# A vision tower with mixture of experts on one core: tokens' join and the first norm's copy on ScalarE, the expert choice ahead of the second differences, and another order in the last block

## The chip, the core and the metric

The kernel runs on one core of a Trainium2 chip. The core has five engines that run beside each other, each with its own queue of instructions: PE (TensorE, matrix products), DVE (VectorE), ACT (ScalarE), POOL (GpSimd) and SP (SyncE, which here only issues DMA transfers). An instruction waits on semaphores until what it reads is there and what it writes is free; everything behind it on the same engine then waits too. The metric is the device time of one execution in microseconds (us); lower is better. The time before is the median of three executions, 2139.51 us (2135.47 to 2140.91).

## The reference

The input is 4 images of 64 channels x 512 steps x 64 columns. A tokenizer makes 16384 tokens of 256 features; an attention-like block with a decaying sum over time and a small perceptron follows, then a layer of 8 experts of which each token takes two.

```python
def _L0_tok_ref(x, W):
    ...
    xf = jnp.fft.rfft(patches, axis=-2, norm='ortho')
    ...
    x_emb = jnp.concatenate([x_real, x_imag], axis=-1)
    x_emb = x_emb @ W.T

def _L0_attn_ref(x, ...):
    h = _layernorm(x, ln1_g, ln1_b)
    q = h @ Wq.T + bq
    k = h @ Wk.T + bk
    v = h @ Wv.T + bv
    def step(mem, inp):
        kv_t, q_t = inp
        mem = decay * mem + kv_t
        return (mem, q_t * mem)
    ...
    x = x + ret
    h2 = _layernorm(x, ln2_g, ln2_b)
    mlp = relu(h2 @ W1.T + b1) @ W2.T + b2
    return x + mlp

def _moe(tokens, router_w, w1, b1, w2, b2):
    probs = softmax(tokens @ router_w.T)
    rw, re = jax.lax.top_k(probs, TOP_K)          # two of eight
    rw = rw / jnp.maximum(rw.sum(-1, keepdims=True), 1e-12)
    out = tokens
    for e in range(E):
        h = gelu(tokens @ w1[e] + b1[e])
        out = out + combine[:, e:e + 1] * (h @ w2[e] + b2[e])

h = _L0_tok_ref(x, W)
h = h + _L0_attn_ref(_layernorm(h), ...)
h = h + _moe(_layernorm(h), ...)
```

## The kernel before

**Blocks.** The tokens are worked on in 32 blocks of 512 (`NB`, `BLK`; the last one's index is `NS` = 31). A block passes through three stages, and one turn of the main loop holds three blocks: `new` = block i, `mid` = block i − 1, `old` = block i − 2.

- `new`: `embed` makes 20 products of five difference planes `xv` with the folded tokenizer weights `wu` (L391) and combines them to `h` on DVE; it then makes two norms of `h` with the same statistics, `zz` (normalized twice, what the projections read) and `z` (normalized once, what the residual adds to), both on DVE by `Norm.apply` (L287, four instructions of 128x256 each). `zz` is turned to feature order `hT`, then `qkv` makes the projections with seven products each for q, k and v (a Strassen-Winograd scheme: `mix_tokens` on DVE makes sums of token halves, L488 to L491; the products are L504, L519 and L520). `scan` runs the decaying sum on DVE (L566, L567, L577), `residual` transposes it back on PE (L588) and adds `z` (L591).
- `mid`: `features2` joins its turned tokens on ACT, `mlp_in` (L334, ACT's relu L620) and `mlp_out` (L630) are the perceptron, and the last norm gives `tok`.
- `old`: `rows` writes the tokens and their numbers as rows (ACT, L678), `turn3` and `join3` turn them to `tokT`, `logits` (L703) scores the experts, `choose` (L727 to L746) picks two of them on DVE, `place` counts the places (PE, L773) and makes the shares (L751 to L754), and `scatter` sends each row to its two experts' regions of a buffer in HBM (POOL, L796). `store` writes the block to the output.

**Turning.** `Turn.split` makes two planes of 16-bit halves on ACT (L313), `start` issues a transposing DMA on SP (L321) into the tile `turned`, and `join` puts the halves together with four copies of 128x512 16-bit elements (L327). `turned` and `planes` have a single buffer: a transfer for the next turn waits until the join before it is done. The first `EARLY` = 6 blocks and the last one turn `zz` with PE's transposes (L300) instead.

**Differences.** The five planes `xv` of the block after `new` are made on DVE by the generator `differences` (L363, L366) in two parts: before its first `yield` four instructions, and then five more. In the loop both parts stand at m = 5 of the perceptron's eight steps, around `features1` and `mix_tokens`. The block after that is loaded into `xb`, a single buffer, by `load_x` on SP.

**Tiles.** A tile is 256 routed rows of one expert. In each turn a few tiles go through their expert between the steps of the blocks ("slots"): SP loads weights, turned rows and shares; ACT puts the rows together (`turn`, L972); PE multiplies twice (`enter`, L979, with gelu on ACT, L987, and `leave`, L996); DVE adds the bias and scales (`sums`, L1008 to L1015, into `y`, four buffers); POOL adds the result to the output with two indirect accumulating transfers a tile (L1025), each waiting for the last two before it to land. After the loop only tiles remain, and the last block's tokens go through all experts densely (L1058 to L1089).

**Order.** The engines PE, DVE, ACT and SP run their instructions in the order in which the program writes them; the order on POOL follows from dependencies. At the turn of the main loop (L1153 on) `join3` stands ahead of the eight steps `mlp_in`; at m = 1 `new.split1()` follows; after the eight steps `logits` and `choose` come, the steps of `qkv` with a tile between them, `place`, `scan`, `mlp_out(0)`, `residual` and `mlp_out(1)`. Blocks 29 to 31 end in a section of its own behind the loop, where `last` is block 31, with its tiles taken by `expert_step` and `expert_halves`.

Of the kernel before, what the change touches and what calls it, by code (L numbers as in the profile page):

```python
# [20 lines left out]
P = 128  # L21
# [15 lines left out]
def vit_tower_kernel(  # L37
# [203 lines left out]
    def mix_weights():  # L241
# [5 lines left out]
        nc.vector.tensor_tensor(t4, w[:, :, 1, 0], t2, ALU.subtract)  # L247
        nc.vector.tensor_tensor(w[:, :, 0, 1], w[:, :, 1, 1], w[:, :, 0, 1], ALU.subtract)

    class Norm:  # L250


# [92 lines left out]
    class Block:  # L345
# [34 lines left out]
        def embed(self):  # L380


            xv = self.xv.rearrange("p i (j w) n -> p i j (w n)", j=J)
            self.h = three.tile([P, TT, D], F32, name="h")
            h = [self.h[:, t, :] for t in range(TT)]

            def products(which):
                ps = p_tm.tile([P, 2, D], F32, name="tm")
                for n, i in enumerate(which):
                    for j in range(J):  # L390
                        nc.tensor.matmul(  # L391
                            ps[:, n, :], lhsT=xv[:, i, j, :], rhs=wu[:, i, j, :], start=j == 0, stop=j == J - 1
                        )
                return ps

            def scaled(to, a, by, b, op):
                nc.vector.scalar_tensor_tensor(to, a, by, b, ALU.mult, op)

            ab = emb.tile([P, 2, D], F32, name="ab")
            nc.scalar.copy(ab, products((1, 2)))  # L400
            a, b = ab[:, 0, :], ab[:, 1, :]
            p, q = h[0], h[3]
            scaled(p, b, 1.0 / 3, a, ALU.add)
            scaled(q, b, -1.0 / 3, a, ALU.add)
            yield
            ps = products((3, 0))
            c, m0 = ps[:, 0, :], ps[:, 1, :]
            norm = Norm()
            scaled(h[2], c, 2.0 / 3, p, ALU.subtract)
            scaled(h[1], c, 1.0 / 3, q, ALU.subtract)  # L410
            scaled(h[0], m0, 0.5, p, ALU.subtract)
            scaled(h[0], c, 1.0 / 6, h[0], ALU.add)
            scaled(h[3], c, 4.0 / 3, q, ALU.subtract)
            for t in range(TT - 1):
                norm.stats(self.h, t)
            yield
            nc.vector.tensor_tensor(h[3], products((4,))[:, 0, :], h[3], ALU.add)
            norm.stats(self.h, TT - 1)
            norm.factors(twice=True)
            yield  # L420
            self.z = one.tile([P, TT, D], F32, name="z")
            self.zz = one.tile([P, TT, D], F32, name="zz")
            norm.apply(self.zz, self.h, 1)
            norm.apply(self.z, self.h, 0)

        def split1(self):
            if self.i < EARLY:
# [259 lines left out]
            self.turn = Turn()  # L687
            self.turn.start([self.row.bitcast(U16)[:, t, : 2 * D] for t in range(TT)])

        def join3(self):  # L690
            self.tokT = one.tile([P, KD, BLK], F32, name="tokT")
            self.turn.join(self.tokT, nc.vector.tensor_copy)

        def features3(self):
            self.tokT = one.tile([P, KD, BLK], F32, name="tokT")
# [16 lines left out]
        def choose(self):  # L712

            ps = self.lg
            shape = [P, TT, E]

            def wide(a):
                return a.unsqueeze(2).to_broadcast(shape)

            lg = small.tile(shape, F32, name="lg")  # L720
            top = small.tile([P, TT], F32, name="top")
            if self.i == NS:
                first_key = small.tile([P, TT], F32, name="first_key")
            else:
                first_key = self.row.bitcast(F32)[:, :, FIRST]
            turned = small.tile([P, TT, G], F32, name="turned_lg")
            nc.vector.transpose(turned.rearrange("p t g -> p (t g)"), ps.rearrange("p t g -> p (t g)"))  # L727
            nc.vector.tensor_reduce(top, turned[:, :, :E], AX.X, ALU.max)
            nc.vector.tensor_tensor(lg, turned[:, :, :E], wide(top), ALU.subtract)
            key = small.tile(shape, F32, name="key")  # L730
            self.oh = oh = small.tile([P, 2, TT, E], F32, name="oh")
            nc.vector.scalar_tensor_tensor(key, lg, 0.0, key0, ALU.is_equal, ALU.mult)
            nc.vector.tensor_reduce(first_key, key, AX.X, ALU.max)
            nc.vector.tensor_tensor(oh[:, 0], key, wide(first_key), ALU.is_equal)
            nc.vector.scalar_tensor_tensor(lg, oh[:, 0], -3.0e38, lg, ALU.mult, ALU.add)
            second = small.tile([P, TT], F32, name="second")
            nc.vector.tensor_reduce(second, lg, AX.X, ALU.max)
            nc.vector.tensor_tensor(key, lg, wide(second), ALU.is_equal)
            nc.vector.tensor_tensor(key, key, key0, ALU.mult)
            nc.vector.tensor_reduce(top, key, AX.X, ALU.max)  # L740
            nc.vector.tensor_tensor(oh[:, 1], key, wide(top), ALU.is_equal)
            dtype = F32 if self.i == NS else BF16
            self.both = small.tile(shape, dtype, name=f"both_{dtype.name}")
            nc.vector.tensor_tensor(self.both, oh[:, 0], oh[:, 1], ALU.add)
            self.ex = small.tile([P, TT], F32, name="ex")
            nc.gpsimd.tensor_tensor(self.ex, euler, second, ALU.pow)  # L746

        def weights(self, diff, second):

# [374 lines left out]
    def run(steps):  # L1124
        for _ in steps:
            pass

    def expert_step(**how):
        run(expert_halves(**how))
# [19 lines left out]
    with tc.manual_schedule(engines=MANUAL):  # L1149
# [3 lines left out]
        for i in range(NS):  # L1153
# [22 lines left out]
            next(embed, None)  # L1176
            if at["enter"]:
                slot(known, load=False)
            if old:
                old.join3()  # L1180
            for m in range(KH):
                if mid:
                    mid.mlp_in(m)
                if m == 1:
                    new.split1()

                    if at["enter"]:
                        advance("load", at["enter"] + AHEAD - 1)
                    elif known > 1:
                        advance("turn", 2)  # L1190
                if m == TT - 1:
                    slot(known)
                if m == KH // 2 and old:
                    old.store()
                if m == KH - 3:
                    ahead = blocks[i + 1].differences(xs.pop(i + 1))
                    next(ahead)
                    new.features1()
                    if i:
                        new.mix_tokens()  # L1200
                    next(ahead)
            if i == NS - 1:
                slot(known)
            later = iter(())
            if i:
                qkv = new.qkv()
                if old:
                    old.logits()
                    old.choose()
                next(qkv)  # L1210
                next(qkv)
                tile_steps = slot_halves(known, sums=False)
# [3 lines left out]
                    writes = old.place(at_once=False)  # L1216
                    old.scatter(1)
                run(tile_steps)
                if i + 2 < NB:
                    xs[i + 2] = load_x(i + 2)  # L1220
                if old:
                    old.scatter(2, last_product[0])
                next(qkv)
# [1 line left out]
                later = slot_halves(known, load=False)  # L1225
                next(later, None)
                next(qkv)
                for m in range(KD):
                    new.scan(m)
                mid.mlp_out(0)  # L1230
                if old:
                    old.scatter(3, last_product[0])
            else:
                xs[i + 2] = load_x(i + 2)
                for m in range(KD):
                    new.retention(m)
            new.residual()
            run(later)
            if old:
                old.scatter(4, last_product[0])  # L1240
            if i == 0:
                mix_weights()
            else:
                new.split2()
            if at["enter"]:
                advance("load", at["enter"] + AHEAD - 1)
            if mid:
# [15 lines left out]
        next(embed, None)  # L1263
        expert_step()
        weights = load_bank()
        old.join3()
        for m in range(KH):
            mid.mlp_in(m)
            if m in (1, 3, 5, 7):
# [2 lines left out]
                expert_step()  # L1272
            if m == KH - 3:
                last.features1()
                last.mix_tokens()
        next(weights)
        old.logits()
        old.choose()
        expert_step()
        writes = old.place()  # L1280
        next(weights)
        qkv = last.qkv()
        next(qkv)
        next(qkv)
        out_steps = mid.mlp_out_steps(0)
        next(out_steps)
        next(qkv)
        run(out_steps)
        next(weights)
        take(NS - 1, old, writes)  # L1290
        next(qkv)
        next(weights)
        expert_step()
        next(qkv)
        for m in range(KD):
            last.scan(m)
        mid.mlp_out(1)
        expert_step(fetch=False, sums=False)
        joined = last.residual_steps()
        next(joined)  # L1300
        beside = expert_halves(fetch=False, sums=False)
        next(beside)
        mid.features3()
        mid.rows()
        run(beside)
        mid.logits()
        mid.choose()
        advance("sums", at["leave"] - 1)
        expert_step(fetch=False, sums=False)
        writes = mid.place()  # L1310
        run(joined)
        expert_step(fetch=False, sums=False)
        advance("sums", at["leave"] - 1)
        take(NS, mid, writes)

        last.features2()
# [118 lines left out]
```

## Time and profile before

| what | value |
|---|---|
| median of three executions | 2139.51 us |
| the profiled execution: its time, its span | 2141.64 us, 2139.9 us |
| mean granted clock of PE in it | 0.993 |
| one turn of the loop, from one issue of the row transposes to the next (1007.87 to 1070.27) | 62.4 us |
| DVE, L327 `tokT`: 120 copies | 44.1 us, 451 ns each |
| DVE, L287 `z` from `h`: 128 instructions | 44.0 us, 407 ns each |
| ACT, L327 `hT`: 100 copies | 66.2 us, 762 ns each |
| ACT, L663 (identity with scale and bias, 128x256): 124 | 64.0 us, 590 ns each |
| POOL, L1025: 226 accumulating transfers for routed tiles | 386.6 us, 1711 ns each |
| DVE small operation on 128x4, L272 | 0.16 us |
| ACT, loading a function table | 2 times, 1283 ns each |

The profiled execution lies 2.1 us above the median. Its span is what the profiler's records cover; 1.7 us lie around it. A row of the timeline gives the start, the duration from the first to the last instruction of a group, the engine, the line, the output and input, the shape, and in brackets how long the engine had been idle just before it and what released it. Idle time of an engine costs nothing unless the work that sets the end waits for it. The granted clock is 1.00 at full speed.

### The profile page before, as it was taken

Reading aid. Unit: us, or ns where it says so; the run is one execution under the profiler, and the core shown is the slowest. Engines: PE = TensorE matmul, PEld = TensorE weight load, DVE = VectorE, ACT = ScalarE, POOL = GpSimd, SP = SyncE. Lnnn points to the kernel's source line nnn. Section 1 sums busy time; section 2 is a strip of 40 time slices with the busy share of each in tenths; the row PEclk is TensorE's granted clock in tenths of the full one; section 3 lists DMA queues with packets and bytes.
Section 4 is the critical chain, followed back from the end, with each engine's and each line's share of the span. In section 5 each row is a group of like instructions: output and inputs, shape, how many; then the busy total and the mean of one; then the engine's idle time right before and its main releaser. Section 6 shows DMA issues by size and latency. Waiting matters only on the chain.

```text
span 2139.9 us, 30460 instructions
## 1 busy us (share of the span) xinstructions
PE 2080.6 (97%) x9060; PEld 1580.7 (74%) x9060; DVE 1759.5 (82%) x5397; ACT 978.0 (46%) x1732; POOL 893.3 (42%) x769
## 2 busy tenths in 40 slices
PE   8999999999999999999999999999999999999988
PEld 6777677777777777777777777777777777776866
DVE  7888888888888888888888888888888888868544
ACT  1333344554444455444445544444555434554533
POOL 1022334444444444444444444444444444434444
PEclk9999999999999999999999999999999999999999
DMA  4032246776567677666767665676775566785643
GB/s 140 21 107 77 80 117 138 160 156 123 119 154 155 141 161 148 122 133 153 158 137 161 153 117 133 153 156 139 164 150 118 135 150 147 151 219 136 102 60 50
DMA packets 424519, 283.21 MB, mean 132 GB/s; under 512 B 355104, under 2 KB 391072, under 8 KB 420256
## 3 DMA queue, kind: packets, MB, share of 16 engines
q1 hardware_dynamic: 373424, 208.35, 41.6%
q0 software_dynamic: 49632, 67.39, 17.7%
q10 hardware_dynamic: 1296, 5.52, 0.7%
q8 instruction: 71, 1.16, 0.2%
q14 instruction: 96, 0.79, 0.1%
HBM read 118.36 MB, written 86.52 MB: 96 GB/s over the span
## 4 chain that ended last, share of the span: by engine, by line
PE 72%; DVE 16%; DMA 8%; issue 2%; POOL 1%; ACT 0%; SPq 0%; POOLq 0%; DVEq 0%; ACTq 0%
PE tm L630 19%; PE tm L391 12%; PE sums L334 12%; PE tm L996 10%; PE mm L979 8%; DMA turned<-planes 7%; PE sums L504 6%; DVE xv L366 2%; DVE xv L363 2%; DVE hT L327 2%; PE tm L588 1%; DMA out<-y,known 1%; PE tm L1075 1%; PE mm L1058 1%; DMA xh<-xbuf 1%
## 5 line engine op out<-in xcount | busy, mean ns | idle before, releaser
L1025 POOL DMA_INDIRECT out<-y,xg x226 | 386.6, 1711 | 454.6 <-DVE y L1015 258.0
L630 PE MATMUL tm<-w_sb,aT 128*128 128x256 f32 x2048 | 454.7, 380 | 0.0
L334 PE MATMUL sums<-hT,w_sb 128*128 128x512 f32 x1024 | 450.2, 592 | 0.0
L630 PEld LDWEIGHTS tm<-w_sb,aT 128*128 128x128 f32 x2048 | 386.7, 190 | 56.4 <-DVE z L591 4.5
L334 PEld LDWEIGHTS sums<-hT,w_sb 128*128 128x128 f32 x1024 | 194.1, 190 | 216.4 <-issue 205.2
L796 POOL DMA_INDIRECT xbuf<-row,to x248 | 245.6, 990 | 230.1 <-DVE row L754 89.1
L313 ACT COPY planes<-zz 128x1024 uint16<-128x1024 uint16 x100 | 99.6, 1043 | 451.4 <-DVE zz L287 451.4
L391 PE MATMUL tm<-wu,xv 128*128 128x256 f32 x1280 | 282.5, 379 | 0.0
L391 PEld LDWEIGHTS tm<-wu,xv 128*128 128x128 f32 x1280 | 242.7, 190 | 32.7
L996 PE MATMUL tm<-w,ge 128*128 128x256 f32 x1048 | 254.4, 386 | 6.8 <-DVE y L1013 6.8
L979 PE MATMUL mm<-xT,w 128*128 128x256 f32 x1048 | 249.9, 382 | 0.0
L979 PEld LDWEIGHTS mm<-xT,w 128*128 128x128 f32 x1048 | 200.1, 191 | 40.8 <-issue 14.5
L620 ACT ACTIVATE aT<-sums,vec 128x512 f32<-128x512 f32 x256 | 171.9, 683 | 117.4 <-PE sums L334 115.7
L996 PEld LDWEIGHTS tm<-w,ge 128*128 128x128 f32 x1048 | 196.1, 191 | 39.0 <-issue 10.5
L972 ACT COPY xT<-xh 128x512 uint16<-128x512 uint16 x262 | 182.3, 768 | 31.1 <-DMA xh<-xbuf 29.9
L987 ACT ACTIVATE ge<-mm,w 128x256 f32<-128x256 f32 x262 | 109.7, 474 | 153.3 <-PE mm L979 117.1
L278 POOL TENSOR_SCALAR rstd<-mv 128x4 f32<-128x4 f32 x62 | 42.0, 677 | 318.9 <-DVE mv L259 292.2
L1013 DVE TENSOR_TENSOR y<-tm,w 128x512 f32<-128x512 f32 x131 | 90.6, 691 | 45.7 <-PE tm L996 41.3
L504 PE MATMUL sums<-hT,wqkv_sb 128*128 128x256 f32 x372 | 110.7, 379 | 0.0
L258 DVE BATCH_NORM_STATS2 st<-h 128x6 f32<-128x256 f32 x256 | 104.8, 409 | 3.3
L366 DVE TENSOR_TENSOR xv<-xb 128x512 f32<-128x512 f32 x160 | 104.1, 683 | 3.1 <-DMA xb<-in_x 3.1
L327 ACT COPY hT<-turned 128x512 uint16<-128x512 uint16 x100 | 66.2, 762 | 81.4 <-DMA turned<-planes 81.4
(218 smaller groups left out, 3029.6 us busy)
## 6 DMA issues: line engine op xcount, KB each, us to landing
w<-in_wex SPq DMA_DIRECT2D x113, 641.5 KB
xb<-in_x SPq DMA_DIRECT2D x32, 1040.0 KB
out<-h SPq DMA_DIRECT2D x31, 512.0 KB
bank<-in_wex ACTq DMA_DIRECT2D x8, 641.5 KB
xbuf<-row,to POOLq DMA_INDIRECT x248
out<-y,xg POOLq DMA_INDIRECT x226
xh<-xbuf SPq DMA_TRANSPOSE x131
xg<-xbuf SPq DMA_DIRECT2D x131, 4.0 KB
```

What stands on the lines that cost most here:

```text
L334: nc.tensor.matmul(ps, lhsT=w[:, k, ts(m, P)], rhs=rhs[:, k, :], start=k == 0, stop=k == KD - 1)
L366: nc.vector.tensor_tensor(to, a, b, ALU.subtract)
L391: nc.tensor.matmul(ps[:, n, :], lhsT=xv[:, i, j, :], rhs=wu[:, i, j, :], start=j == 0, stop=j == J - 1)
L504: nc.tensor.matmul(g[:, n, :], lhsT=lhsT, rhs=rhs, start=False, stop=True, skip_group_check=True)
L620: nc.scalar.activation(self.aT[:, m, :], ps, AF.Relu, bias=vec[:, MB1 + m : MB1 + m + 1])
L630: last_product[0] = nc.tensor.matmul(ps[:, i, :], lhsT=self.aT[:, k, ts(u * 2 + i, P)], rhs=w2_sb[:, k, :], start=k == 0, stop=k == KH - 1,)
L796: write = nc.gpsimd.indirect_dma_start(out=xbuf, out_offset=bass.IndirectOffsetOnAxis(ap=self.to[:, c, t : t + 1], axis=0), in_=self.row[: ...
L972: nc.scalar.copy(halves[:, :, :, 1 - i], self.xh[:, i * KD : (i + 1) * KD, :])
L979: nc.tensor.matmul(ps[:, m, :], lhsT=self.w[:, k * D + m * P : k * D + (m + 1) * P], rhs=self.xT[:, k, :], start=k == 0, stop=k == KD - 1,)
L987: nc.scalar.activation(self.ge[:, m, :], ps[:, m, :], AF.Gelu, bias=self.w[:, 5 * D + m : 5 * D + m + 1])
L996: last_product[0] = nc.tensor.matmul(ps[:, c, :], lhsT=self.ge[:, k, ts(c, P)], rhs=w[:, (2 + k) * D : (3 + k) * D], start=k == 0, stop=k ...
L1025: add = nc.gpsimd.indirect_dma_start(out=out, out_offset=bass.IndirectOffsetOnAxis(ap=number[:, c, :], axis=0), in_=y[:, c, :], in_offset= ...
```

## The change

The change has five parts.

1. `join3` takes the copy as an argument. In the loop it is ACT's; the call moves from ahead of the eight steps to m = 1, ahead of `split1` (for i from `EARLY` on), or to m = 4, ahead of `store` (before that). The section behind the loop keeps DVE's.
2. `embed` makes `zz` on DVE as before, and in place of `z` one small operation for −mean/deviation; the new `first_norm` makes `z` with four ACT instructions, after the steps of `qkv`.
3. `next(ahead)`, the second part of the differences, moves from m = 5 to behind `choose` (i from `EARLY` on) or behind `residual` (0 < i < `EARLY`); the loads of `xb` move along in the program.
4. `choose` of the last block takes the exponential with ACT's function instead of POOL's power.
5. The last block makes its projections with `retention`, which block 0 uses too: four products for each half of the features instead of the seven, on weights whose last mixing step `restore_weights` undoes. `mix_tokens` is left out there, and the tile steps, `mlp_out` and the residual of the ending stand in another order.

```diff
+    def restore_weights():
+        w = wqkv_sb.rearrange("p w k (m q) -> p w k m q", q=P)
+        nc.vector.tensor_tensor(w[:, :, 0, 1], w[:, :, 1, 1], w[:, :, 0, 1], ALU.subtract)
...
             norm.apply(self.zz, self.h, 1)
-            norm.apply(self.z, self.h, 0)
+            self.first = norm
+            self.shift = small.tile([P, TT], F32, name="shift")
+            nc.vector.scalar_tensor_tensor(
+                self.shift, norm.mv[:, :, 0], -1.0, norm.rstd[:, 0, :], ALU.mult, ALU.mult
+            )
+
+        def first_norm(self):
+            for t in range(TT):
+                nc.scalar.activation(
+                    self.z[:, t, :],
+                    self.h[:, t, :],
+                    AF.Identity,
+                    bias=self.shift[:, t : t + 1],
+                    scale=self.first.rstd[:, 0, t : t + 1],
+                )
...
-        def join3(self):
+        def join3(self, copy):
             self.tokT = one.tile([P, KD, BLK], F32, name="tokT")
-            self.turn.join(self.tokT, nc.vector.tensor_copy)
+            self.turn.join(self.tokT, copy)
...
-            nc.gpsimd.tensor_tensor(self.ex, euler, second, ALU.pow)
+            if self.i == NS:
+                nc.scalar.activation(self.ex, second, AF.Exp)
+            else:
+                nc.gpsimd.tensor_tensor(self.ex, euler, second, ALU.pow)
...
-            if old:
-                old.join3()
             for m in range(KH):
                 if mid:
                     mid.mlp_in(m)
                 if m == 1:
+                    if old and i >= EARLY:
+                        old.join3(nc.scalar.copy)
                     new.split1()
...
                 if m == KH // 2 and old:
+                    if i < EARLY:
+                        old.join3(nc.scalar.copy)
                     old.store()
                 if m == KH - 3:
                     ahead = blocks[i + 1].differences(xs.pop(i + 1))
...
                     if i:
                         new.mix_tokens()
-                    next(ahead)
+                    else:
+                        next(ahead)
...
                     old.choose()
+                if i >= EARLY:
+                    next(ahead)
                 next(qkv)
...
                 next(qkv)
+                new.first_norm()
                 for m in range(KD):
                     new.scan(m)
+                if EARLY <= i < NB - 2:
+                    xs[i + 2] = load_x(i + 2)
...
             new.residual()
+            if 0 < i < EARLY:
+                next(ahead)
...
                 last.features1()
-                last.mix_tokens()
...
         writes = old.place()
         next(weights)
-        qkv = last.qkv()
-        next(qkv)
-        next(qkv)
-        out_steps = mid.mlp_out_steps(0)
-        next(out_steps)
-        next(qkv)
-        run(out_steps)
+        restore_weights()
+        last.first_norm()
+        last.retention(0)
+        mid.mlp_out(0)
         next(weights)
         take(NS - 1, old, writes)
-        next(qkv)
         next(weights)
-        expert_step()
-        next(qkv)
-        for m in range(KD):
-            last.scan(m)
         mid.mlp_out(1)
-        expert_step(fetch=False, sums=False)
-        joined = last.residual_steps()
-        next(joined)
-        beside = expert_halves(fetch=False, sums=False)
+        last.retention(1)
+        beside = expert_halves(fetch=False)
         next(beside)
         mid.features3()
         mid.rows()
-        run(beside)
+        advance("leave", at["enter"] - 1)
         mid.logits()
         mid.choose()
-        advance("sums", at["leave"] - 1)
+        run(beside)
         expert_step(fetch=False, sums=False)
         writes = mid.place()
-        run(joined)
+        advance("sums", at["leave"])
         expert_step(fetch=False, sums=False)
-        advance("sums", at["leave"] - 1)
+        last.residual()
+        expert_step(fetch=False, sums=False)
+        advance("sums", at["leave"])
+        expert_step(fetch=False)
         take(NS, mid, writes)
```

More of the change, by code (lines that the diff above doesn't have):

```diff
@@ L1218, in vit_tower_kernel @@
                 run(tile_steps)
-                if i + 2 < NB:
-                    xs[i + 2] = load_x(i + 2)
                 if old:
@@ L1234, in vit_tower_kernel @@
                 xs[i + 2] = load_x(i + 2)
+                new.first_norm()
                 for m in range(KD):
@@ L1244, in vit_tower_kernel @@
                 new.split2()
+            if 0 < i < EARLY:
+                xs[i + 2] = load_x(i + 2)
             if at["enter"]:
@@ L1265, in vit_tower_kernel @@
         weights = load_bank()
-        old.join3()
+        old.join3(nc.vector.tensor_copy)
         for m in range(KH):
```

## The prediction

> **What bounds the kernel now.** I read the page's busy times first, then the list of waits over the whole span, then one block of the loop engine by engine, then the end on POOL.
>
> ```profile
> span 2139.9 us, 30460 instructions
> PE 2080.6 (97%) x9060; PEld 1580.7 (74%) x9060; DVE 1759.5 (82%) x5397; ACT 978.0 (46%) x1732; POOL 893.3 (42%) x769
> ```
>
> PE is busy for 97% of the span: a faster step elsewhere is worth only the time in which PE stands still for it. The waits (engine, line, releaser; total us, times, longest) price these:
>
> ```profile
> DVE hT L327 <- DMA turned<-planes: 41.4, 25, 3.2
> PE tm L773 <- DVE both_bfloat L744: 15.6, 26, 1.7
> DVE share L751 <- POOL ex L746: 9.5, 1, 9.5
> PE tm L996 <- DVE y L1013: 6.8, 1, 6.8
> PE mm L520 <- DVE planes L488: 5.9, 17, 0.5
> ```
>
> PE waits 15.6 us in 26 blocks for the expert choice (L744), and 5.9 us for token sums that follow the join of hT; with the window cut to 56 to 1850 us, L519 adds 4.1 us in 5 blocks for hT itself. The two waits of 9.5 and 6.8 are one event at 2046. The timelines of one block (start, duration, instruction, then the idle before it) show the order that makes the waits:
>
> ```profile
> 1017.87 1.46 DVE L327 COPY tokT<-turned 128x512 uint16<-128x512 uint16 x4
> ...
> 1024.92 1.47 DVE L327 COPY hT<-turned 128x512 uint16<-128x512 uint16 x4 [1.36 <-DMA turned<-planes]
> ...
> 1027.97 1.28 DVE L366 TENSOR_TENSOR xv<-xb 128x512 f32<-128x512 f32 x2
> ...
> 1034.03 0.19 DVE L744 TENSOR_TENSOR both_bfloat<-oh 128x32 bf16<-128x32 f32 x1
> ```
>
> ```profile
> 1034.27 0.20 PE L773 MATMUL tm<-both_bfloat,rc 128*128 128x32 bf16 x2 [0.56 <-DVE both_bfloat L744]
> ```
>
> DVE makes the second half of the differences (1027.97 to 1031.2) before the choice (1031.22 to 1034.2), and PE arrives 0.56 us too soon. SP and ACT in the same block:
>
> ```profile
> 1007.87 5.13 SPq L321 DMA_TRANSPOSE turned<-row  x4
> 1019.39 3.31 SPq L321 DMA_TRANSPOSE turned<-planes  x1
> ```
>
> ```profile
> 1003.35 2.65 ACT L327 COPY hT<-turned 128x512 uint16<-128x512 uint16 x4 [2.88 <-DMA turned<-planes]
> ...
> 1015.13 1.99 ACT L313 COPY planes<-zz 128x1024 uint16<-128x1024 uint16 x2 [2.49 <-DVE zz L287]
> ```
>
> The planes were ready at 1017.12, but their transpose went out at 1019.39, just after DVE's tokT join: both use the single buffer `turned`. The end is POOL's:
>
> ```profile
> 1965.33 1.60 POOL L1025 DMA_INDIRECT out<-y,xg  x1 [0.30 <-DVE from_row L874]
> ...
> 2132.44 1.58 POOL L1025 DMA_INDIRECT out<-y,known  x1 [2.72 <-DVE zz L1083]
> ```
>
> Between these two lie 24 intervals of accumulate pairs, (2132.44 − 1965.33)/24 = 6.96 us each; the span ends 5.9 us after the last one starts.
>
> **Choice ahead of the second differences.** Nothing is added. The choice is 2.95 us long and the differences 3.25 (1027.97 to 1031.22), so L744 comes 3.25 us sooner against a longest wait of 1.7: the wait goes whole in the blocks from EARLY on. Late next is the place chain, which stands behind the differences on DVE: L773's result has 2.4 us of small operations before L540 at 1037.27, where DVE waited 0.36 for PE, so it fits within some 0.3 us. Scatters follow `place` on POOL and the following load of xb stands on SP at 1039.35, after both halves are made in either order. Value −15.0 (bounds −15.6 and −9, the last if each of 25 blocks keeps a quarter of a microsecond).
>
> **Early blocks.** In blocks 1 to 5 the second half moves behind the residual, where 3.25 us of DVE work delay the norm zz, and with it PE's transposes L300. Before, such transposes lost 4.0 us once up to 400 us. PE has other products queued ahead, and I take 0.3 a block, +1.5; bounds 0 and 5 x 3.25 = 16.3.
>
> **tokT join on ACT.** DVE loses four copies of 1.47 us in all. ACT gains four like the join of hT that it does already, 2.65 us. They stand after aT(1) (ends 1012.65) and ahead of the planes' copies. When are the rows there? DVE's join did not wait at 1017.87, which bounds the landing from above; the last issue ends at 1013.0. The windows of one microsecond (PE, PEld, DVE, ACT, POOL busy, clock, then DMA share and GB/s) say more:
>
> ```profile
> 1013.00:1014.00 1.00, 1.00 (x4) 0.48 (x3) 0.34 (x2) 0.00 (x0) 0.63 (x1) 1.00 0.64 130
> 1014.00:1015.00 1.00, 1.00 (x4) 0.47 (x3) 1.00 (x5) 0.00 (x0) 0.00 (x0) 1.00 0.00 0
> ```
>
> Packets stop at 1014, so with a little for the notice the copies run from 1014.3 to 1016.95. Planes follow to 1018.95, and SP issues at about 1019.0, 0.4 before the 1019.39 of today. Bounds: rows already there at 1012.65 leave the planes waiting for zz (1015.04), and SP issues at 1017.35, 2.0 sooner; rows there only at 1017.87 give 1020.5, 1022.5 and SP 3.2 later. I take the value by the DMA row, the nearest. In hT that is 0.3 to 0.4 us in each of the 17 blocks where L520 waited 0.35 on average; against it stand blocks where zz comes sooner than the rows and the issue slips. Value −3 of 10.0 us; bounds −10 and 25 x 3.2 = +80, the last a rival. aT(2) is next behind the planes on ACT: it would end at 18.95 + 0.69, 1019.65; the three sums buffers make m = 5 wait for it, and those products begin at 1018.64 + 1.72 = 1020.36. The cover is 0.7 us.
>
> **First norm on ACT.** DVE loses four of 0.41 (1.37 together) and gains one small operation of about 0.16 like L272. ACT gains four like L663, 2.07 us, from 1042.6 where it is idle until 1058; their reader L591 comes after the scans. Value 0; without that cover 2.07 x 31 = 64 us. Both moves free DVE of 31 x (1.37 + 1.47 − 0.16) = 83 us, worth nothing by themselves, and bring ACT from 978 to 978 + 31 x (2.65 + 2.07) = 1124, 53%.
>
> By the rows, moving this work costs 31 x (1.18 + 0.70) = 58 us of engine time and none of PE's. A rule speaks against it: the Trainium skill, "ScalarE: Activation LUTs", section "Rules for kernel authors", gives plain adds and products to VectorE. Its reason, that VectorE is faster for each element, is true of the rows: 1.47 against 2.65 us, 1.37 against 2.07. Taken as time on the path it would turn the sum below to plus 40; with ACT at 46% and DVE at 82% ahead of PE's waits, I go by the waits.
>
> **Ending.** Exp on ACT instead of POOL's pow takes away the 6.8 us at 2046 and the half clock around it (a mean of 0.51 from 2043 to 2050), but in that stretch POOL's accumulates, not PE, set the end: 0, or −10 if they did not. It brings two table loads; the trace's row for one is 1.28 us, 2.6 together, under the same cover. By the same page ("What ACT_TABLE_LOAD costs") a switch is 2.66 with its drain, and two would be 5.3; no run here shows a switch in mid kernel. In the last block twelve products of 128x512 at 0.86 (10.3) replace 21 of 128x256 at 0.43 (9.1). Two tile steps of 3.45 and some transposes leave the stretch from the first `place` to the second, 42.5 us today (1908.27 to 1950.77). In the new order I count 10.3 + 13.8 (64 rows of L630) + 1.7 + 1.6 + 1.7 + 0.6 + 1.7 + 1.7 = 33.1 us. So the second scatter comes about 9 us sooner, but one more pair of 6.96 stands behind it: −2. If it instead waits 3.5 us for zz or xT before `place` (such waits of 2.5 and 1.3 stand at 1957 and 1960 now), +1.5; a scatter not earlier at all, +7; a pair that finds its slot free, −7.
>
> **Sum.** −15.0 + 1.5 − 3.0 + 0 − 2.0 = −18.5 on the profiled execution (2139.9 and 1.7 around the span, 2141.6): 2123.1. It stood 2.1 above the median 2139.51, so the forecast is 2121.
>
> **Rivals.** *Eaten*: hT slips by 0.56 a block, as if the copies began 1 us later (rows noticed at 1015.3), 25 x 0.56 = 14: −15 + 14 + 1.5 − 2 = −1.5, 2138. For it: blocks with rows late against zz exist, and earlier accumulates on POOL may meet the transposes' packets. Against: packets end at 1014. *Slower*: the ACT join waits for the rows until past 1016, and planes, SP issue and hT all slip by 1.2 us or more: 25 x 1.2 = 30 (the 0.9 by which aT(2) then outruns its cover is part of it, since PE stands still once for both); −15 + 30 + 1.5 − 2 = +14.5, 2154. It decides from 0.8 us of slip on (−15.5 + 25 x 0.8 = +4.5); the spread of landings decides, and there is one buffer. It can grow by the clock: where the wait reached 1.4 us, the granted clock from 525 to 530 and 1714 to 1719 averaged 0.75 and 0.66; a like stretch in each of 25 blocks, 3.4 us at half speed, would add 25 x 1.7 = 42. *More*: every L519/L520 wait goes too (10.0), the ending keeps 7, early blocks cost nothing: −15.6 − 10 − 7 = −33, 2107. *The choice is not ahead in fact*: the order on DVE is written by hand, so the new program has it; no chance apart.
>
> **How the numbers follow.** Forecast 0.61 (its own range 2112 to 2133), more 0.12, eaten 0.11, slower 0.16. A measurement here tells 0.3%, 6.4 us, from no change. Faster is forecast and more, 0.73; same 0.11; slower 0.16. Range 2108 to 2143: it leaves out the slower case and the lowest few of "more".
>
> **What would show it.** L773's wait under 1 us in all; DVE L327 left with hT alone; ACT's tokT join starting 6 to 7 us after the row transposes' issue; SP's planes transpose at 11.0 us after it, not 11.5; PE waits on hT and planes of 10 us or less; 26 accumulate pairs behind the last scatter, whose end lies near 1956 less the loop's gain. Wrong it would be if the ACT join waits on DMA turned<-row beyond 8 us after the issue, if aT shows as a PE releaser, or if half-clock stretches multiply.

## The result and the profile after

The changed kernel takes 2116.78 us (median of four runs, 2116.49 to 2117.79) against 2138.84 of the kernel before (four runs beside it): a ratio of 0.9899, with a 95% interval of 0.9882 to 0.9916. The profiled execution took 2116.5 us, 25.2 less than that of before.

The page of the changed kernel, its span and the busy times:

```profile
span 2114.7 us, 30454 instructions
...
PE 2077.4 (98%) x9042; PEld 1576.0 (75%) x9042; DVE 1674.8 (79%) x5179; ACT 1100.8 (52%) x1966; POOL 886.9 (42%) x768
```

DVE lost 85 us of work, ACT gained 123, and PE's busy time is nearly what it was: the gain is idle time of PE. The list of PE's waits between 56 and 1835 us (line, releaser: us in total, times, longest):

```profile
PE mm L539 <- ACT ge L1010: 3.0, 1, 3.0
PE mm L540 <- DVE planes L508: 2.9, 7, 0.6
PE mm L539 <- DVE hT L332: 1.4, 1, 1.4
PE mm L305 <- DVE zz L292: 1.3, 1, 1.3
PE sums L339 <- ACT aT L640: 1.3, 3, 0.5
```

The wait for the choice (L773 before, L796 now) is gone from the list, the waits for hT and its sums (L539, L540; L519 and L520 before) fell from 10.0 to 4.3 us, and two small new ones came, zz and aT. The wait for gelu stood in before too (1.6 us at 1846, outside this window) and grew to 3.0. The same turn of the loop as shown of before, on DVE, ACT and SP (start, duration, instruction, idle before it):

```profile
1003.74 1.38 DVE L292 TENSOR_SCALAR zz<-h,mv,rstd 128x256 f32<-128x256 f32 x4 [1.84 <-POOL rstd L288]
...
1014.99 1.49 DVE L332 COPY hT<-turned 128x512 uint16<-128x512 uint16 x4 [2.10 <-DMA turned<-planes]
...
1020.86 0.19 DVE L764 TENSOR_TENSOR both_bfloat<-oh 128x32 bf16<-128x32 f32 x1
1020.97 1.28 DVE L371 TENSOR_TENSOR xv<-xb 128x512 f32<-128x512 f32 x2
```

```profile
1004.81 2.64 ACT L332 COPY tokT<-turned 128x512 uint16<-128x512 uint16 x4 [2.12 <-DMA turned<-row]
1007.31 1.98 ACT L318 COPY planes<-zz 128x1024 uint16<-128x1024 uint16 x2
```

```profile
998.31 5.14 SPq L326 DMA_TRANSPOSE turned<-row  x4
1009.32 1.68 SPq L326 DMA_TRANSPOSE turned<-planes  x1
```

The choice now ends at 1021.0, and PE's place product comes at 1023.64 without a wait. ACT's join starts 6.5 us after the first row transpose is issued and waits 2.12 us for the rows; SP issues the planes' transpose 11.0 us after the rows, as forecast, against 11.5 in the turn shown of before (median of 22 turns: 10.99 against 11.28). DVE now waits 2.1 us for that transfer where it waited 1.36.

Where the time went, from the start of PE's place product in each turn (turn n lies between the products n and n + 1) and of the accumulate pairs on POOL:

| stretch | before, us | after, us | difference |
|---|---|---|---|
| to the first place product | 130.4 | 130.2 | −0.2 |
| turns 1 to 5 (early blocks) | 277.7 | 277.1 | −0.6 |
| turns 6 to 27 | 1378.0 | 1354.4 | −23.6 |
| turn 28 (block 30) | 66.4 | 70.3 | +3.9 |
| turn 29 | 55.8 | 55.5 | −0.3 |
| from there to the first pair behind the last scatter | 57.1 | 49.7 | −7.3 |
| from there to the end of the span | 174.6 | 177.6 | +3.0 |

Turn 28 is what the expectations below call turn 30. Of the 23.6 us of turns 6 to 27, 7.0 lie in two turns of before in which PE waited 1.38 and 1.14 us for hT and then had a stretch of 3.4 us at half speed; the other twenty turns fell by 0.83 us on average. The last two rows are the ending: the first pair starts sooner, and one pair more follows. POOL's timeline of the changed kernel at these two points:

```profile
1937.13 1.59 POOL L1048 DMA_INDIRECT out<-y,xg  x1 [0.30 <-DVE tile_share L1031]
...
2105.96 1.56 POOL L1048 DMA_INDIRECT out<-y,known  x1 [3.01 <-DVE zz L1106]
```

25 intervals of 6.75 us lie between them, against 24 of 6.96. Turn 28 is the one place that got worse. ACT and SP there:

```profile
1805.46 2.63 ACT L332 COPY tokT<-turned 128x512 uint16<-128x512 uint16 x4 [3.30 <-DMA turned<-row]
...
1821.92 1.38 ACT L995 COPY xT<-xh 128x512 uint16<-128x512 uint16 x2 [4.58 <-DMA xh<-xbuf]
```

```profile
1797.68 5.14 SPq L326 DMA_TRANSPOSE turned<-row  x4
1809.96 3.00 SPq L326 DMA_TRANSPOSE turned<-planes  x1
...
1815.45 1.27 SPq L972 DMA_TRANSPOSE xh<-xbuf  x1
```

The rows came 1.3 us later than usual, so join, copies and the planes' issue (12.3 after the rows) slipped, and with them the next tile's transposes, which stand behind on SP. This turn has one tile more than the others, and its products wait 3.0 us for gelu (1.6 before). The granted clock then fell to a half for 3.4 us from 1825; from 1825 to 1829 its mean is 0.57.

### The profile page after: what moved, and what is told of

It reads as the page before. It is cut to its first block, busy times and chain, and to the rows that moved or that the text cites. A ratio compares the mean times of both kernels' runs of the same rounds, so it can differ in the third digit from the quotient of the medians.

```text
span 2114.7 us, 30454 instructions
## 1 busy us (share of the span) xinstructions
PE 2077.4 (98%) x9042; PEld 1576.0 (75%) x9042; DVE 1674.8 (79%) x5179; ACT 1100.8 (52%) x1966; POOL 886.9 (42%) x768
## 4 chain that ended last, share of the span: by engine, by line
PE 74%; DVE 11%; ACT 5%; DMA 5%; issue 2%; POOL 2%; SPq 1%; another core or an unknown queue 0%; ACTq 0%; DVEq 0%; POOLq 0%
PE tm L650 17%; PE sums L339 13%; PE tm L396 9%; PE sums L524 9%; PE mm L1002 8%; PE tm L1019 8%; DMA turned<-planes 3%; DVE st L263 2%; PE mm L540 1%; ACT planes L318 1%; ACT tokT L332 1%; PE tm L1098 1%; PE mm L1081 1%; PE mm L539 1%; SPq L326 1%
## 5 line engine op out<-in xcount | busy, mean ns | idle before, releaser
L1048 POOL DMA_INDIRECT out<-y,xg x226 | 369.2, 1634 | 432.7 <-DVE y L1038 220.2
L819 POOL DMA_INDIRECT xbuf<-row,to x248 | 257.1, 1037 | 294.3 <-DVE ks L560 170.5
L640 ACT ACTIVATE aT<-sums,vec 128x512 f32<-128x512 f32 x256 | 167.0, 690 | 60.6 <-PE sums L339 59.3
L332 ACT COPY hT<-turned 128x512 uint16<-128x512 uint16 x100 | 66.2, 762 | 80.5 <-DMA turned<-planes 80.5
L332 ACT COPY tokT<-turned 128x512 uint16<-128x512 uint16 x116 | 76.5, 760 | 58.7 <-DMA turned<-row 58.7
```

Source lines behind the costliest of these rows:

```text
L332: copy(to[:, 1 - i], self.turned[:, :, i, k, :])
L640: nc.scalar.activation(self.aT[:, m, :], ps, AF.Relu, bias=vec[:, MB1 + m : MB1 + m + 1])
L819: write = nc.gpsimd.indirect_dma_start(out=xbuf, out_offset=bass.IndirectOffsetOnAxis(ap=self.to[:, c, t : t + 1], axis=0), in_=self.row[: ...
L1048: add = nc.gpsimd.indirect_dma_start(out=out, out_offset=bass.IndirectOffsetOnAxis(ap=number[:, c, :], axis=0), in_=y[:, c, :], in_offset= ...
```

## The experiments

Three sets of four kernels, each set on a chip of its own with the kernel before beside it (2135.23, 2130.25 and 2137.20 us), so ratios are compared across sets and times within one.

| run | median, us | ratio to before (95%) | median turn 6 to 27, us | planes' issue after rows', us |
|---|---|---|---|---|
| kernel before | 2138.84 | 1 | 62.32 | 11.28 |
| changed kernel | 2116.78 | 0.9899 (0.9882 to 0.9916) | 61.41 | 10.99 |
| choice alone | 2118.19 | 0.9922 (0.9901 to 0.9943) | 61.60 | 11.28 |
| join back on DVE | 2104.74 | 0.9851 (0.9829 to 0.9873) | 61.09 | 10.04 |
| norm back on DVE | 2113.53 | 0.9900 (0.9878 to 0.9922) | 61.58 | 11.00 |
| ending back | 2117.40 | 0.9915 (0.9895 to 0.9936) | 61.46 | 10.99 |
| changed kernel again | 2111.68 | 0.9915 (0.9898 to 0.9931) | 61.37 | 10.99 |
| join and norm back | 2116.54 | 0.9936 (0.9920 to 0.9953) | 61.50 | 11.29 |
| join later still | 2127.02 | 0.9978 (0.9969 to 0.9988) | 61.84 | 12.13 |
| join and ending back | 2100.29 | 0.9858 (0.9842 to 0.9875) | 61.09 | 10.03 |
| norm alone | 2107.22 | 0.9852 (0.9836 to 0.9869) | 61.15 | 10.06 |
| norm and choice | 2100.35 | 0.9828 (0.9812 to 0.9845) | 61.09 | 10.06 |
| join back, power back | 2102.58 | 0.9834 (0.9818 to 0.9850) | 61.09 | 10.05 |
| join and early back | 2101.68 | 0.9829 (0.9812 to 0.9845) | 61.09 | 10.03 |

**The choice alone**, an edit of the kernel before:

```diff
                         new.mix_tokens()
-                    next(ahead)
+                    if i < EARLY:
+                        next(ahead)
...
                     old.choose()
+                if i >= EARLY:
+                    next(ahead)
                 next(qkv)
```

> The kernel before with one edit: from block 6 on, the second half of the differences behind the choice. My theory (the choice's wait alone): L773's 15.6 us shrink to the 3.6 of blocks 1 to 5, so 12.0 us less than before, 2127 against a before of 2139; L519 and L520 keep their 10.0 us. Rival (the 83 us taken from DVE are what made room): without them the place chain and L540 come late behind the differences, the gain stays under 5 us, 2134 or more, and L504 or L566 show new waits.

It gained 17.0 us, more than my 12 and far from the rival's 5. PE's waits over the whole span:

```profile
PE mm L520 <- DVE planes L488: 6.0, 17, 0.5
PE mm L519 <- DVE hT L327: 4.7, 5, 1.6
PE tm L773 <- DVE both_bfloat L744: 3.3, 3, 1.7
```

The waits at hT stand as they were, and only early ones at the choice are left. So the choice needs nothing of what was taken from DVE. Why 17 and not 12: the turn of before shows it, in PE's timeline just ahead of the place product at 1034.27:

```profile
1032.69 0.59 PE L504 MATMUL sums<-hT,wqkv_sb 128*128 128x256 f32 x2
1033.12 0.59 PE L504 MATMUL sums<-planes,wqkv_mix 128*128 128x256 f32 x2
```

These pairs start 0.43 us apart, so the next product could have started at 1033.55; it started at 1034.27, 0.72 later. The list of waits has 0.56, because it counts idle time only from the modelled end of a product that overlaps the next. The median turn fell by 62.32 − 61.60 = 0.72. In the profile, turns 6 to 27 fell by 17.1 us: 14.0 in twenty turns, and 3.1 in the two turns that had a stretch at half speed before and have none here.

**The join back on DVE**, an edit of the changed kernel:

```diff
                 slot(known, load=False)
+            if old:
+                old.join3(nc.vector.tensor_copy)
             for m in range(KH):
...
                 if m == 1:
-                    if old and i >= EARLY:
-                        old.join3(nc.scalar.copy)
                     new.split1()
...
                 if m == KH // 2 and old:
-                    if i < EARLY:
-                        old.join3(nc.scalar.copy)
                     old.store()
```

> The changed kernel with the tokens' join back on DVE at its old place. My theory: SP issues the planes' transpose 0.3 us later in most blocks and PE's waits at hT and its sums go from 4.3 back to about 10, +5.7; against it turn 30, where the rows came late for ACT, gets some 3 us back and aT's 1.3 us go: 2117 + 2 = 2119 (2117 to 2121). Rival (DVE's time): 44 us of copies on DVE bring waits at the choice back, 2125 or more.

Both expectations fell: it took 2104.74 us, with a ratio below the changed kernel's interval. Its page and one turn on DVE, SP and PE:

```profile
PE 2071.5 (98%) x9042; PEld 1578.3 (75%) x9042; DVE 1722.7 (82%) x5295; ACT 1036.1 (49%) x1850; POOL 885.7 (42%) x768
```

```profile
1005.48 1.46 DVE L332 COPY tokT<-turned 128x512 uint16<-128x512 uint16 x4
...
1012.55 1.46 DVE L332 COPY hT<-turned 128x512 uint16<-128x512 uint16 x4 [0.76 <-DMA turned<-planes]
```

```profile
996.95 5.13 SPq L326 DMA_TRANSPOSE turned<-row  x4
1007.00 3.29 SPq L326 DMA_TRANSPOSE turned<-planes  x1
```

```profile
1014.99 0.70 PE L539 MATMUL mm<-hT,wqkv_sb 128*128 128x256 f32 x2
```

DVE has 48 us more to do than in the changed kernel, and the kernel is faster. With z no longer in front of it, the tokens' join on DVE starts 8.5 us after the rows' issue, where it started 10.0 after in the turn shown of before, and SP issues the planes at 10.05: 1.0 sooner than by way of ACT, whose 2.6 us of join and 2.0 of planes stand in series behind the rows. In the changed kernel the joined hT is ready about when PE gets there, with no room; here it is ready at 1014.01 and PE's first product of it comes at 1014.99, about 1 us of room, and 20 of the turns 6 to 27 last 61.09 us, a floor that no turn of any run went below by more than 0.02. Turn 28 lasts 64.6 instead of 70.3, since one more tile is all that it has.

**The norm back on DVE**, and **the ending back**, each an edit of the changed kernel:

```diff
-            self.first = norm
-            self.shift = small.tile([P, TT], F32, name="shift")
...
+            norm.apply(self.z, self.h, 0)
...
-                new.first_norm()
                 for m in range(KD):
                     new.scan(m)
```

```diff
-        restore_weights()
-        last.first_norm()
-        last.retention(0)
-        mid.mlp_out(0)
+        qkv = last.qkv()
+        next(qkv)
...
+        last.first_norm()
+        for m in range(KD):
+            last.scan(m)
...
```

> The changed kernel with z's norm back on DVE in embed. My theory: 1.2 us later on DVE, against 2.7 us of room ahead of the place product and an hT join that waits 2 us for its DMA: no change, 2117 within 1. Rival (DVE's time is what counts): +38 us x a part, 2122 or more.

> The changed kernel with the order and the products of the ending before (seven products in the last block), Exp staying on ACT. My theory: the first accumulate pair after the second scatter stands 7.3 us later after the first place, one pair fewer follows, and the span grows by the 4.3 us that the ending gave: 2121. Rival (the pair eats it): 2117 within 1.

The norm back: 0.9900 against 0.9899, no difference that could be measured. In the changed kernel, then, the norm's place is worth nothing that the time shows: SP waits for ACT's join there and not for DVE, and issues at 11.00 either way. The profile is less even than the time. PE's waits at hT and its sums rose from 4.3 to 8.2 us:

```profile
PE mm L536 <- DVE planes L504: 5.3, 11, 0.5
PE mm L535 <- DVE hT L332: 2.9, 7, 0.6
```

Turns 6 to 27 became 5.0 us longer together, and turn 28 was 4.1 shorter (66.2). The ending back: 0.9915, inside the interval of the changed kernel, and the profiled span 0.8 longer (2115.5). The 7 us by which the first pair came sooner are taken back by the additional pair, so the ending gave nothing that these runs resolve. From the place product at which those last two rows begin to the end of the span, the six profiled executions with the old ending took 223.0 to 231.6 us and the eight with the new one 223.8 to 228.5; the kernel before was the longest of them, which is why the table above shows a gain.

**The changed kernel again, join and norm both back, and the join later still.** The second combines the two diffs above; the third makes `split1` only copy the planes and issues their transpose (`go`) after the join, with the next tile's loads still behind it:

```diff
                 if m == 1:
-                    if old and i >= EARLY:
-                        old.join3(nc.scalar.copy)
                     new.split1()
...
+                if m == 2 and i >= EARLY:
+                    old.join3(nc.scalar.copy)
+                    new.turn.go()
```

> The changed kernel itself, for a comparison with its variants on one chip: 2117 by its own runs, 2113 if the chip of the last four runs was faster (its kernel before had 2135 against 2139).

> The changed kernel with the join and the first norm both back on DVE. Theory A (what counts is how soon SP can issue the planes' transpose; z on DVE stands ahead of the tokens' join there): SP at 11.3 us after the rows' issue as with the choice alone, waits at hT and its sums near 10 again, the loop 6.7 longer than in the changed kernel, turn 30 some 4 shorter: 2 to 3 above the changed kernel. Theory B (the join on ACT is what costs, the norm is neutral): equal to the run with the join back, 12 below the changed kernel.

> The changed kernel with planes' copies first on ACT, then aT(2), then the tokens' join and only then the planes' transpose, with the next tile's loads behind it as before. Theory A: SP issues at 12.0 instead of 11.0, hT has no room left, so PE waits about 1 us more in each of 24 turns, +22 to +26 us, more where a wait draws a stretch at half clock. Theory B (ACT's load, which is the same here, counts and not the path): under +5.

The changed kernel took 2111.68 here. Join and norm back stands 4.9 us above it: the theory of SP's issue had the sign and the turns (61.50, issue at 11.29, waits of 9.1 us at hT and its sums), the theory of ACT's load is refuted. So what the norm's move is worth depends on where the join stands: with the join on DVE 0.9936 against 0.9851, some 18 us; with the join on ACT 0.9900 against 0.9899, nothing. The later join stands 15.3 above: again the theory of the issue, but well below its price of 22 to 26. PE's waits there, and the transfer:

```profile
PE mm L544 <- DVE planes L512: 11.1, 24, 0.5
```

```profile
1003.57 5.14 SPq L330 DMA_TRANSPOSE turned<-row  x4
1015.84 2.87 SPq L330 DMA_TRANSPOSE turned<-planes  x1
```

```profile
1020.94 1.47 DVE L336 COPY hT<-turned 128x512 uint16<-128x512 uint16 x4 [2.53 <-DMA turned<-planes]
```

PE now waits for the sums 24 times, at most 0.5 us each. Of the 15.7 us between the two profiled spans, 9.3 lie in turns 6 to 27 and 2.9 in turns 1 to 5. The issue came 1.1 us later, but hT only 0.5, because the transfer took 5.1 us here (median 5.0) instead of 5.6. Why a later transfer is shorter, these runs don't show.

**Join and ending back** combines the two edits of the changed kernel.

> The run with the join back on DVE, and the ending before in place of the older one. If the ending gave what its first pair's start says (7.3 sooner, a pair of 6.8 more): 1 us above the run with the join back, 2105 to 2106. If PE's 4.3 in the ending count: 2109.

0.9858 against 0.9851: as expected, the ending does nothing here either.

**The norm alone, and the norm with the choice**, edits of the kernel before:

```diff
-            norm.apply(self.z, self.h, 0)
+            self.first = norm
+            self.shift = small.tile([P, TT], F32, name="shift")
...
                 next(qkv)
+                new.first_norm()
                 for m in range(KD):
                     new.scan(m)
```

> The kernel before with one edit: z's first norm on ACT after the projections, as in the change. What I put on record for it is nothing. Theory A (z stood on DVE ahead of the tokens' join and so ahead of SP's issue): planes go out at 10.1 us after the rows instead of 11.3, hT comes 1.2 sooner, its 10 us of waits go, and the choice behind it comes 1.2 sooner against a wait of 0.56 in 21 turns, so turns fall from 62.2 to about 61.1 and the whole by some 22 us, to 0.990 of before. Rival (the choice's wait stays, as its place is the same): 10 us, 0.9955. Rival (nothing, as on record): 1.000.

> The kernel before with two edits: the first norm on ACT, and the second half of the differences behind the choice from block 6 on; join, early blocks, Exp and ending as before. Theory A: turns at PE's floor of 61.09 as with the join back, so 0.986 to 0.988 of before, and within 5 us of the first norm alone, since both edits take the same waits. Rival (the two add up): 12 to 17 us below the first norm alone.

The norm alone is worth 30.0 us, more than the whole change and more than the 22 of theory A. In the profile 27.1 lie in turns 6 to 27, whose median of 61.15 is what theory A had, and 3.5 in turns 1 to 5. PE's waits between 56 and 1835, and DVE and SP in one turn:

```profile
PE tm L788 <- DVE both_bfloat L759: 2.8, 5, 0.6
PE mm L535 <- DVE planes L503: 1.2, 3, 0.5
```

```profile
998.30 0.15 DVE L426 SCALAR_TENSOR_TENSOR shift<-mv,rstd 128x4 f32<-128x4 f32 x1
...
999.99 1.46 DVE L327 COPY tokT<-turned 128x512 uint16<-128x512 uint16 x4
...
1016.23 0.19 DVE L759 TENSOR_TENSOR both_bfloat<-oh 128x32 bf16<-128x32 f32 x1
```

```profile
991.29 5.14 SPq L321 DMA_TRANSPOSE turned<-row  x4
1001.51 3.30 SPq L321 DMA_TRANSPOSE turned<-planes  x1
```

Taking 1.2 us out in front of the tokens' join moves all that follows on DVE and SP forward: the planes go out at 10.2, hT is early (PE waits for it once, 0.2 us), and even the choice, still behind the second differences, mostly ends in time (1016.4; PE's place product came at 1016.50). With the choice moved too the turns are at 61.09 and the ratio is 0.9828, 6.9 us below the norm alone (theory A had at most 5, the rival 12 to 17): the two edits take mostly the same waits and don't add up.

**Power back and early blocks back**, both on the run with the join back:

```diff
-            if self.i == NS:
-                nc.scalar.activation(self.ex, second, AF.Exp)
-            else:
-                nc.gpsimd.tensor_tensor(self.ex, euler, second, ALU.pow)
+            nc.gpsimd.tensor_tensor(self.ex, euler, second, ALU.pow)
```

```diff
                     if i:
                         new.mix_tokens()
-                    else:
+                    if i < EARLY:
                         next(ahead)
...
-            if 0 < i < EARLY:
-                next(ahead)
```

> The run with the join back, and the last block's exponential on POOL's power again. If POOL's accumulates set the end there, as on record: within 1.5 us of the run with the join back (0.985 of before). Rival (PE's wait of 6.8 and the half clock around it count): 5 us or more above it, 0.988.

> The run with the join back, and the second half of the differences of blocks 1 to 5 at their old place. Theory: 3.3 us of the choice's waits return in those blocks, 1.5 us at zz and 1.8 with a half-clock stretch at 340 go, so within 1.5 us of the run with the join back (0.985). Rival (the early blocks' order matters): 3 us or more either way.

Neither costs: 2102.58 and 2101.68 in one set, by ratio 3.6 and 4.7 us below the run with the join back, with intervals that overlap. The power on POOL brings back no loss that shows at the end. The early blocks' old order makes turns 1 to 5 shorter by 3.5 us (274.1 against 277.6 with the new order), of which 0.9 is left between the two medians, too little to resolve.

**A version faster than both kernels.** The norm with the choice, two small edits of the kernel before, is at 0.9828 (0.9812 to 0.9845), against 0.9899 and 0.9915 for the changed kernel. Join back with early blocks back (0.9829) and with the power back (0.9834) can't be told from it; the interval of join back alone overlaps too.

## Why the prediction was right, and where its steps were off

The forecast was 2121 us with a range of 2108 to 2143; 2116.8 lies in it, and faster was the likely case. That the total came so near is in part luck: turns 6 to 27 gave 23.6 us where the sum had some 14.5, and turn 28 took back 3.9 that the sum did not have. By its steps:

- **The bound.** Right. PE stood still for the choice, for hT and for its sums, and the time came out of these waits.
- **Choice ahead of the second differences, −15.0.** The mechanism was right and the size too small. The wait went whole, but a turn lost 0.72 us by the cadence of the products where the list said 0.56; over the 21 turns that had this wait that is 3.4, and most of the rest lies in the two turns with a stretch at half speed. The choice alone gave 17.0 with the early blocks left as they were. The loop as a whole gave 20.9 (place product at 1887.4 instead of 1908.3) where the sum had 16.5.
- **Early blocks, +1.5.** The sum counted their waits at the choice in the −15.0, so it had about −2 for them. They gave 0.6. PE waited 1.3 us for zz once, as feared. Once the norm is on ACT, the old order is better there by 3.5 us in the profiles.
- **tokT join on ACT, −3.** Against the kernel before, the instants were right: start 6.5 us after the rows' issue, SP at 11.0, hT 0.3 sooner, waits from 10.0 to 4.3, more than the −3 of the sum. But the comparison was the wrong one. With the norm off DVE, leaving the join on DVE gives SP at 10.05; as part of this change the join's move costs 10 to 14 us (0.9851 against 0.9899 and 0.9915). The cover of 0.7 us for aT was real: when rows came late, PE waited for it three times, 1.3 us together. aT as a releaser of PE was named as a sign of being wrong; it came in these three turns alone.
- **First norm on ACT, 0, and the 83 us of DVE "worth nothing by themselves".** This is the step that failed. Within the changed kernel its value is 0 in time, as the run with the norm back shows. By itself it is worth 30 us, and some 20 with the choice already moved (0.9828 against 0.9922). z stood on DVE ahead of the tokens' join, that join frees the buffer for which SP's transpose waits, and that transpose sets hT. I had used this chain in the step before and did not apply it to what stands ahead of the join.
- **Ending, −2.** Within the profiled pair it gave 7.3 − 3.0 = 4.3, but the same ending varies by more than that between runs; by the runs with the ending back, nothing resolved. Both are inside the bounds of that step (−7 to +7).
- **Exp.** Two loads of 1.28 us came, under cover, as costed. The prediction says that no run shows a switch in mid kernel; the trace of before has a load at 270.49.
- **Rivals.** "Slower" named the right place: the join on ACT waits for rows, in turn 28 and four others 0.6 us or more beyond the usual, and turn 28 lost some 5.7 us against its floor of 64.5. But the usual landing left the path as computed. The later join tests that rival's price: hT ended 0.5 us later there (18.6 after the rows' issue against 18.1) and the turn grew by 0.47, so each microsecond of hT's slip does cost one a turn; but of 1.1 us of slip at SP only that half arrived at hT.

The rule weighed there, from the Trainium skill ("ScalarE: Activation LUTs", "Rules for kernel authors": plain adds and products belong on VectorE), was read as speaking against both moves. The join is a copy, which that row does not list; at 2.6 us on ACT and 1.5 on DVE it is better on DVE here, because it lies on the path to SP's issue. The norm, a product and a sum, takes 2.1 and 1.4 and is better on ACT by 30 us in the kernel before, because it no longer stands ahead of that join and nothing waits for it where it went. Speed alone would have decided the norm wrongly. Of the same page's price for a table switch, 2.66 us with its drain, the trace shows the 1.28 of the load alone: Exp ran from 2008.43, right after the load of 2007.14, and the load for gelu began 0.01 after the copy in between; the load at 270.49 began 0.01 after the instruction before it.

## What to carry to other kernels

Before an edit that frees an engine is costed at nothing, follow what stands behind the freed slot on that engine, up to the issue of the next transfer: 1.2 us a turn ahead of a join that released a buffer was worth 30 us here, and nothing once that join stood on another engine. Cost each part of a change also against the change without it; parts that shorten the same wait don't add up, and one can undo another. On a pipelined engine read a loss from the spacing of the starts, not from the idle column, which was 0.16 us a turn too low.

## What the runs showed of the hardware

Whether a wait on PE is followed by a stretch at half clock does not go by its length alone. Turns with waits of 1.38 and 1.14 us at hT were followed by 3.4 us at half speed before (at 527 and 1715); the changed kernel had one of 1.4 us (near 585) with none after it, and one of 3.0 us with 3.4 at half. In the run with the choice alone, waits of 1.58 and 1.19 us at hT (at 526 and 1699) had none after them. The prediction gave both waits of before as 1.4. The transpose of the same planes took 5.6 us when issued 10.0 to 11.3 us after the rows and 5.0 at 12.1 (medians of 22 turns).
